# Weaving two batches of a Fourier-layer kernel: chains of one batch between bulk units of the other

## The chip, the cores and the metric

The kernel runs on one core of a Trainium2 chip. The metric is the device time of one execution in microseconds (us); lower is better. The median of three runs before the change is 803.64 us (803.38 to 805.07). All data are 32-bit floats.

Names used below: PE is the matrix engine (TensorE), PEld its weight loads, DVE the vector engine, ACT the scalar (activation) engine, POOL is GpSimd, SP the engine whose queue issues most DMAs. PSUM is the memory that PE writes its products to: 8 banks of 512 floats on each of 128 partitions. SBUF is the main on-chip memory.

## The reference

The input `x` has 2 batches of 56 channels, each a plane of 128 x 128. Two layers of the same form follow one another, with weights of their own:

```
x = x + layer(group_norm(x))

layer(x):                                   # 56 planes of a batch are "tokens"
    xn = instance_norm(x)
    k, q, v = fno(xn, K), fno(xn, Q), fno(xn, V)        # 1 plane -> 8 heads
    attn = softmax(q . k / 128)                          # 56 x 56, each head
    out = fno(attn @ v, P)                               # 8 heads -> 1 plane
    att = instance_norm(out + x);  an = instance_norm(att)
    h = gelu(instance_norm(spectral(an, M0)) + skip)     # exact Gelu
    h = instance_norm(spectral(h, M1)) + skip
    return instance_norm(h) + att

spectral(x, w): rfft2, keep 32 x 16 low modes, multiply by complex w, irfft2
fno(x) = spectral(x) + 1x1 skip
```

Only 32 x 16 complex modes of a plane are kept, so the Fourier transforms are products with small cosine and sine matrices. Attention needs no full planes: the scores come from the modes and from the 56 x 56 Gram matrix of the planes. Full planes are touched where a nonlinearity or a new input needs them: at the load, at the Gelu, and at the end of a layer.

## The kernel before

All work is written out in Python, with no loop left at run time. A compiler pass then orders the instructions of each engine's queue by program order and by its own estimate of when inputs are ready, places tiles, and adds the waits. Each queue runs in order. So the order of the program is a strong hint of the order on an engine, not the order itself.

A batch's `x` stays in SBUF as `X2`: 56 channels on partitions 0 to 55 and, for the other half of the rows, on 64 to 119. `P[b]` holds a batch's working planes. Each stage below runs for one layer `L` and one batch `b`:

- `turned` (line 323): 4 transposes on PE, an ACT copy to `P`, and `bn_stats` on DVE for group statistics; 16 calls turn a batch.
- `modes_stage` (413): group norm from the statistics, the scaling of the plane in four parts (L431 on ACT, L433 on DVE), the transform along the width (L436), a 32 x 32 transpose on DVE (L441), the transform along the height (`to_modes`, L342), the Gram matrix in 128 small products (L460), and square roots for the scores.
- `scale_x` (489): scales `X2` in place for the skip paths (L492 on DVE).
- `heads_stage` (498): scores (L526, L515), softmax, values (L551), attention applied (L596).
- `norms_stage` (607): means and variances of the two instance norms, as sums of squared modes by one-column products (`sums`, L398); then factors, spread over partitions by a product (`rows_of`, L391), the new spectrum (`spectrum`) and the transform back along the height (`inverse`, L358 and L363).
- `gelu_stage` (676): in four blocks, `mixed` rebuilds four tiles of a plane (synthesis along the width L659, 32 products with 64 columns of weights; skip product L669), then Gelu on ACT (L685), the sum of squares on DVE (L686), transposes back (L689), a copy on ACT (L691) and the forward transform (L695).
- `h_stage` (702): modes of the Gelu's output, the second spectral product (`multiply`, L376), its statistics, factors and spectrum, and `inverse`.
- `end_stage` (753): `mixed` again, then for each of 16 tiles a read-back of the layer's input by SP into one of three tiles `xr` (L763), two DVE passes (L765 adds the mixed part, L767 scales by 1/std and adds the read-back), and a store by SP (L769). In layer 0 the result also goes to `X2`, and `turned` starts the next layer.

`prepare` (206) forms the products of the weights on POOL, `relay` (283) turns them, `build` (307, L310) expands them into block matrices on POOL. PSUM has 6 single banks (`bank()`) and one pair, used by `inverse`. `evict` (198) alternates PSUM copies between ACT and DVE. The last lines call the stages: heads and norms of batch 0, then of batch 1; Gelu and `h_stage` of batch 0, then of batch 1; in layer 0 `end_stage` and the next `modes_stage` for each batch in turn, in layer 1 both `end_stage`s. A PE product of 32-bit floats is two instructions in the profile.

Of the kernel before, what the change touches and what calls it, by code (L numbers as in the profile page):

```python
# [26 lines left out]

# [7 lines left out]
F32 = mybir.dt.float32  # L36
# [6 lines left out]
EPS = 1e-5  # L43
# [4 lines left out]
for _name, _n in (  # L48
    ("ident", N), ("fw", 32), ("fh", N), ("gh", 2 * N), ("gw", N), ("group", N), ("dup", N), ("ext", N),
    ("fold", 64), ("raw", 56), ("count", 8), ("syn", 1), ("same", 32), ("m8", 8), ("m16", 16), ("first", 1),  # L50
    ("n2", 1),
):
    _PARTS[_name] = (sum(n for _, n in _PARTS.values()), _n)
# [3 lines left out]
def _constants():  # L57
    pos = np.arange(N)
    rows = 4 * (pos % 32) + pos // 32
    th = 2 * np.pi * np.outer(pos, np.arange(16)) / N  # L60
    ph = 2 * np.pi * np.outer(rows, _KY) / N
    pg = 2 * np.pi * np.outer(pos, _KY) / N
    fw = np.concatenate([np.cos(th), -np.sin(th)], 1) / N
    cy, sy = np.cos(ph), np.sin(ph)
    fh = np.concatenate([cy, -sy, sy, cy], 1) / N
    ghs = []
    for h in (pos.reshape(4, 4, 8), pos.reshape(8, 4, 4)):
        turn = h.transpose(1, 0, 2).reshape(-1)
        cz, sz = np.cos(pg[turn]), np.sin(pg[turn])
        g = np.stack([np.concatenate([cz, -sz], 1).T, np.concatenate([sz, cz], 1).T], 1)  # L70
        ghs.append(np.concatenate([g, g], 0).reshape(N, 2 * N))
# [7 lines left out]
    for r in range(2):  # L79
# [20 lines left out]
        "ident": np.eye(N), "fw": fw, "fh": fh, "gh": ghs[0], "gw": gw, "group": group, "dup": dup, "ext": ext,  # L100
# [6 lines left out]
        "first": (p == 0)[:, None] * 1.0, "n2": np.full((N, 1), 1.0 / N**2),  # L107
    }
    whole = np.concatenate([parts[n] for n in _PARTS] + ghs[1:], 1)
# [23 lines left out]

@with_exitstack
def fno_layers(ctx: ExitStack, tc: tile.TileContext, x, out, weights, small, const):
# [7 lines left out]
    mp = pool("mid", 2)  # L143
# [3 lines left out]
    ps = pool("psum", 6, space=bass.MemoryType.PSUM)  # L147
    pq = pool("pair", 1, space=bass.MemoryType.PSUM)
# [3 lines left out]

    def little(name, shape):
        return sm.tile(shape, F32, name=name)

# [4 lines left out]
    nc.scalar.dma_start(out=ident, in_=const["all"][:, :N])  # L160
    X2 = xp.tile([N, B, 64, N], F32, name="X2")
    xin = x.rearrange("b k (g c r) w -> c b k g (r w)", c=2, r=8)
    for b in range(B):
        for g in range(0, 8, 2):
            V.memset(X2[32:64, b, 8 * g : 8 * g + 16, :], 0.0)
            G.memset(X2[96:128, b, 8 * g : 8 * g + 16, :], 0.0)
# [5 lines left out]
            if (b, g) == (0, 2):  # L172
                nc.scalar.dma_start(out=Ct[:, N:], in_=const["all"][:, N:N_CONST])
# [19 lines left out]
    def grid(flat, n=8):  # L193
        return flat.rearrange("p (t k) -> p t k", t=n)
# [684 lines left out]
```

## Time and profile before

| what | value |
|---|---|
| median of three runs | 803.64 us |
| profiled execution, its own time | 804.52 us |
| its span, first to last instruction | 802.7 us |
| busy: PE, PEld, DVE, ACT, POOL | 563.5, 373.6, 395.9, 189.7, 98.6 us |
| mean granted PE clock | 0.753 |
| moved by DMA | 40.18 MB |

An engine is busy while an instruction of its own runs; the busy times overlap, and their shares of the span are means over stages that are limited by different things. The granted clock is the share of the full PE clock that the chip allowed. A chain line names a step of the chain of work that ended last; "idle before <-" in a group names what ended the wait of the group's engine.

### The profile page before, as it was taken

What the parts mean: (1) busy time and instruction counts of PE and PEld (TensorE: products, weight loads), DVE (VectorE), ACT (ScalarE), POOL (GpSimd) and SP (SyncE); (2) the same over time, 40 slices, a digit from 0 to 9 for tenths busy, and PEclk for the clock granted to TensorE, in tenths of its full rate; (3) what the DMA queues carried; (4) which work ended last, traced back from release to release, by engine and by line L of the source; (5) the groups of instructions that cost most, each with busy time, mean ns of one, the idle gap of its engine ahead of it and who ended that gap; (6) DMA issues with size and microseconds to landing.
All of it is one profiled execution on the core that took longest, in us unless ns stands there. A gap on an engine that the chain in (4) does not pass through costs nothing.

```text
span 802.7 us, 18778 instructions
## 1 busy us (share of the span) xinstructions
PE 563.5 (70%) x8334; PEld 373.6 (47%) x8334; DVE 395.9 (49%) x781; ACT 189.7 (24%) x364; POOL 98.6 (12%) x151
## 2 busy tenths in 40 slices
PE   1576689898797796674476646888979679677810
PEld 1455576867553543432243223767664354353300
DVE  8577813142525344456575556434234434447752
ACT  1405003215044244111111111142324425310000
POOL 9900088000000001400000000000000000000000
PEclk9886859598579589557686667997968959858855
DMA  7920110000000000034403341000000000004565
GB/s 190 209 39 1 30 39 2 2 3 2 0 2 2 2 1 2 1 99 141 136 3 95 107 145 27 4 2 2 2 2 2 2 1 2 2 1 148 181 203 168
DMA packets 21664, 40.18 MB, mean 50 GB/s; under 512 B 4304, under 2 KB 5072, under 8 KB 21584
## 3 DMA queue, kind: packets, MB, share of 16 engines
q1 hardware_dynamic: 20576, 36.98, 16.4%
q10 hardware_dynamic: 1008, 2.01, 0.9%
q8 instruction: 65, 1.06, 0.6%
q14 instruction: 15, 0.12, 0.1%
HBM read 24.03 MB, written 14.68 MB: 48 GB/s over the span
## 4 chain that ended last, share of the span: by engine, by line
PE 47%; DVE 24%; ACT 10%; DMA 9%; issue 5%; SPq 4%; POOL 0%; DVEq 0%; ACTq 0%; POOLq 0%
PE bank L669 7%; PE bank L659 5%; PE bank L526 4%; DVE X L492 4%; PE bank L398 4%; DMA xr<-store 4%; PE pair L358 3%; DMA X<-x 3%; PE bank L596 3%; PE bank L695 3%; PE bank L300 3%; PE bank L342 3%; DVE X L767 2%; DMA xr<-x 2%; DVE P L765 2%
## 5 line engine op out<-in xcount | busy, mean ns | idle before, releaser
L326 PE MATMUL bank<-C,X 120*128 120x120 f32 x256 | 46.6, 341 | 67.2 <-DVE X L767 41.1
L669 PE MATMUL bank<-X,Bs 57*64 57x512 f32 x512 | 91.8, 771 | 0.0
L326 PEld LDWEIGHTS bank<-C,X 120*128 120x128 f32 x256 | 36.7, 182 | 82.8 <-issue 58.0
L686 DVE SCALAR_TENSOR_TENSOR bank<-P 128x512 f32<-128x512 f32 x64 | 42.8, 719 | 50.8 <-ACT P L685 50.6
L329 ACT COPY P<-bank 128x448 f32<-128x448 f32 x64 | 32.9, 541 | 126.3 <-PE bank L326 125.4
L765 DVE SCALAR_TENSOR_TENSOR P<-P,der,bank 128x512 f32<-128x512 f32 x64 | 44.6, 742 | 17.1 <-PE bank L669 17.0
L685 ACT ACTIVATE P<-bank 128x512 f32<-128x512 f32 x64 | 35.4, 601 | 63.8 <-PE bank L669 63.8
L334 DVE BATCH_NORM_STATS2 stats<-P 128x6 f32<-128x448 f32 x64 | 37.7, 620 | 23.0 <-ACT P L329 23.0
L526 PE MATMUL bank<-xf,WU 64*64 64x56 f32 x1024 | 42.2, 247 | 0.0
L526 PEld LDWEIGHTS bank<-xf,WU 64*64 64x64 f32 x1024 | 39.4, 160 | 6.0 <-issue 5.3
L659 PE MATMUL bank<-C,mid 32*64 32x128 f32 x1024 | 35.1, 371 | 8.4 <-DVE P L765 8.4
L203 DVE COPY P<-bank 128x448 f32<-128x448 f32 (+1 forms) x32 | 20.3, 653 | 40.8 <-PE bank L526 40.8
L767 DVE SCALAR_TENSOR_TENSOR P<-P,r,xr 128x512 f32<-128x512 f32 x32 | 23.8, 750 | 31.1 <-DMA xr<-store 31.0
L669 PEld LDWEIGHTS bank<-X,Bs 57*64 57x64 f32 x512 | 21.6, 166 | 37.2 <-issue 37.2
L689 PE MATMUL bank<-C,P 120*128 120x120 f32 x256 | 37.0, 278 | 0.0
L492 DVE TENSOR_TENSOR X<-X,gvr 120x1024 f32<-120x1024 f32 x32 | 36.8, 1213 | 0.3
L691 ACT COPY WT<-bank 128x448 f32<-128x448 f32 x64 | 32.6, 535 | 17.2 <-PE bank L689 17.0
L689 PEld LDWEIGHTS bank<-C,P 120*128 120x128 f32 x256 | 26.3, 142 | 21.1 <-ACT P L685 15.6
L659 PEld LDWEIGHTS bank<-C,mid 32*64 32x64 f32 x1024 | 25.0, 180 | 21.8 <-DVE P L765 14.1
L436 PE MATMUL bank<-P,C 128*32 128x448 f32 x128 | 22.3, 808 | 18.0 <-DVE P L433 17.9
L695 PE MATMUL bank<-WT,C 128*32 128x112 f32 x512 | 25.5, 271 | 13.2 <-ACT WT L691 12.4
L201 ACT COPY P<-bank 128x448 f32<-128x448 f32 (+1 forms) x32 | 17.0, 558 | 68.9 <-PE bank L526 58.6
(229 smaller groups left out, 908.3 us busy)
## 6 DMA issues: line engine op xcount, KB each, us to landing
X<-x SPq DMA_DIRECT2D x16, 448.0 KB
xr<-x SPq DMA_DIRECT2D x64, 112.0 KB
store<-X SPq DMA_DIRECT2D x64, 112.0 KB
xr<-store SPq DMA_DIRECT2D x64, 112.0 KB
out<-P SPq DMA_DIRECT2D x64, 112.0 KB
mid<-weights ACTq DMA_DIRECT2D x2, 544.0 KB
C<-const_all ACTq DMA_DIRECT2D x1, 557.5 KB
X<-gvr SPq DMA_DIRECT2D x8, 32.0 KB
```

The source lines that it names most:

```text
L326: T.transpose(p[:, N * e : N * e + 120], X2[:120, b, 8 * g + 4 * s + e, :], ident[:120, :120])
L334: V.bn_stats(stats[:, 2 * g + s, :], v)
L492: V.tensor_tensor(v, v, _bc(st["gvr"][:120], 1, 8), ALU.mult)
L526: T.matmul(two[k][64 * e : 64 * e + 64, K * a : K * a + K], lhsT=WUv[64 * e : 64 * e + 64, t + k, a, :], rhs=xv[64 * e : 64 * e + 64, t + ...
L659: T.matmul(four[j][64 * c : 64 * c + 64, N * e : N * e + N], lhsT=Z[32 * j : 32 * j + 32, o : o + 64], rhs=C["gw"][32 * j : 32 * j + 32, : ...
L669: T.matmul(four[2 * v + r][64 * c : 64 * c + 64, :], lhsT=Bs[q, :], rhs=X2[q, b, s : s + 4, :].rearrange("p e w -> p (e w)"), start=False, ...
L685: S.activation(h3, four[j], AF.Gelu)
L686: V.scalar_tensor_tensor(four[j], h3, 1.0, h3, ALU.mult, ALU.mult, accum_out=ec[:, n : n + 1])
L689: T.transpose(p[:, N * e : N * e + 120], h3[:120, N * e : N * e + N], ident[:120, :120])
L695: T.matmul(dst, lhsT=C["fw"], rhs=t[:, q], start=(j == 0), stop=True, tile_position=(0, 32 * q), skip_group_check=True,)
L765: V.scalar_tensor_tensor(h3, h3, d["gm1"], four[j], ALU.mult, ALU.add)
L767: V.scalar_tensor_tensor(dst, h3, st["r3"], back, ALU.mult, ALU.add)
```

## The change

The stages become Python generators which yield the estimated PE cost of what they have just issued. `_woven(lead, bulk)` runs a chain of short dependent steps (the lead) and, after each step, issues units of bulk work until their costs add up to what the step yielded. The leads and bulks are, in order: the modes of batch 0 with the turn of batch 1; the modes of batch 1 with the Gram product of batch 0; the rest of Gram and norms of one batch with the Gram product or the scores of the other; the softmax with the values; the mixing with the heads; the norms of batch 0 with all attention of batch 1; the norms of batch 1 with the Gelu of batch 0; `h_chain` of batch 0 with the Gelu of batch 1; `h_chain` of batch 1 with the `end` of batch 0; in layer 0 the modes of layer 1 with the `end` of batch 1.

Besides: PSUM becomes 2 single banks and 3 pairs of banks, and tiles double to 1024 columns (2 x 448 or 2 x 512); all PSUM copies of the bulk go to ACT, two of the four plane scalings too. Synthesis uses 128 columns of weights (`Z` padded to 64 columns a row), 16 products instead of 32 in each block. In layer 0 the turn transposes each half of the channels by itself, so the empty partitions of `X2` need no zeros; they are filled from `x` at the end of the load. Weights and constants are loaded first, on ACT's queue. In `norms_chain` one of three sums of squares goes away. The Gelu's statistics come from `bn_stats`. The layer's last 1/std goes into the factors that precede it (`dcq`, `Be`, `D`, `hs`), so that DVE makes one pass in `end` and POOL adds the read-back. Read-backs are issued two tiles ahead; in the last `end` all eight go ahead, into `X2` of batch 0.

```diff
+def _woven(lead, *bulks):
+    rest = chain(*bulks)
+    for want in lead:
+        while want > 0:
+            cost = next(rest, None)
+            if cost is None:
+                break
+            yield cost
+            want -= cost
+    yield from rest
...
-    ps = pool("psum", 6, space=bass.MemoryType.PSUM)
-    pq = pool("pair", 1, space=bass.MemoryType.PSUM)
+    ps = pool("psum", 2, space=bass.MemoryType.PSUM)
+    pq = pool("pair", 3, space=bass.MemoryType.PSUM)
...
-            V.memset(X2[32:64, b, 8 * g : 8 * g + 16, :], 0.0)
-            G.memset(X2[96:128, b, 8 * g : 8 * g + 16, :], 0.0)
...
+    for b in range(B):
+        nc.sync.dma_start(out=X2[K:64, b], in_=x[b, :8, :64, :])
...
-            if j == 1:
+            if j % 2:
                 S.activation(v, v, AF.Identity, bias=sh, scale=gv)
...
+    def synthesis(A, both, Z):
+        for e in range(4):
+            for j in range(4):
+                o = 64 * (8 * A + 2 * e)
+                T.matmul(
+                    both[j // 2][:, j % 2, N * e : N * e + N], lhsT=Z[32 * j : 32 * j + 32, o : o + N],
+                    rhs=C["gw"][32 * j : 32 * j + 32, :], start=(e == 0), stop=False, tile_position=(32 * j, 0),
+                    skip_group_check=True,
+                )
...
+    def gelu(L, b, st):
...
+        for A in range(6):
+            if A < 4:
+                both = [pair(), pair()]
+                synthesis(A, both, st["Z"])
+                yield 1.0
+            if A > 1:
+                forward(A - 2, 1)
+                yield 0.4
+            for v in range(2):
+                if A < 4:
+                    mixed(L, b, A, v, both[v], st["Bs"])
+                    h3 = at(A, v)
+                    S.activation(h3, both[v].rearrange("p r m -> p (r m)"), AF.Gelu)
+                    for r in range(2):
+                        V.bn_stats(stats[:, 4 * A + 2 * v + r, :], h3[:, 512 * r : 512 * r + 512])
+                    yield 0.9
+                if 0 < A < 5:
+                    turn_back(A - 1, v)
+                    yield 0.8
+            if 0 < A < 5:
+                forward(A - 1, 0)
+                yield 0.4
...
+    def end(L, b, st, stats):
...
+        for n in range(8 if ahead else 2):
+            load(n)
+        late = []
         for A in range(4):
+            both = [pair(), pair()]
+            synthesis(A, both, st["Z"])
+            yield 1.0
+            for v in range(2):
+                n = 2 * A + v
+                mixed(L, b, A, v, both[v], st["Be"])
+                h3 = P[b][:, 1024 * n : 1024 * n + 1024]
+                V.scalar_tensor_tensor(h3, h3, st["hs"], both[v].rearrange("p r m -> p (r m)"), ALU.mult, ALU.add)
+                dst = X2[:, b, 8 * n : 8 * n + 8, :].rearrange("p e w -> p (e w)") if L == 0 else h3
+                G.tensor_tensor(dst, h3, back(n), ALU.add)
+                moved(dst, to, A, v, True, nc.sync)
+                if not ahead:
+                    load(n + 2)
+                yield 0.9
+                late.append(n)
+                if L == 0 and len(late) > 2:
+                    turned(b, late.pop(0), 1, stats)
+                    yield 0.8
...
+        _run(_woven(modes_chain(L, 1, ...), gram(0, s0)))
+        _run(_woven(gram_chain(L, 0, s0), _with(gram(1, s1), scale_x(0, s0))))
+        _run(_woven(gram_chain(L, 1, s1), scores(L, 0, s0)))
+        _run(_woven(softmax_chain(L, 0, s0), values(L, 0, s0)))
+        _run(_woven(mix_chain(L, 0, s0), heads(L, 0, s0)))
+        _run(_woven(
+            norms_chain(L, 0, s0), _with(scores(L, 1, s1), scale_x(1, s1)),
+            _woven(softmax_chain(L, 1, s1), values(L, 1, s1)), _woven(mix_chain(L, 1, s1), heads(L, 1, s1)),
+        ))
+        _run(_woven(norms_chain(L, 1, s1), gelu(L, 0, s0)))
+        _run(_woven(h_chain(L, 0, s0), gelu(L, 1, s1)))
+        _run(_woven(chain(h_chain(L, 1, s1), more), end(L, 0, s0, stats[0])))
+        if L == 0:
+            _run(_woven(modes_chain(1, 0, stats[0], st[1][0]), end(0, 1, s1, stats[1])))
+        else:
+            _run(end(1, 1, s1, None))
```

746 lines of the change are left out of this document (395 added, 351 removed).

## The prediction

> **What bounds the kernel now.** I read the page's engine rows and clock row first, then the shares of the chain, the groups by line, the chain in order of time, and last the busy time by stretch. In the engine rows and the chain's shares no engine is full:
>
> ```profile
> PE 563.5 (70%) x8334; PEld 373.6 (47%) x8334; DVE 395.9 (49%) x781; ACT 189.7 (24%) x364; POOL 98.6 (12%) x151
> PE 47%; DVE 24%; ACT 10%; DMA 9%; issue 5%; SPq 4%; POOL 0%; DVEq 0%; ACTq 0%; POOLq 0%
> ```
>
> PE is busy for 70% of the span and carries under half of the chain; DVE carries 24%, ACT 10% and DMA 9%. So time is lost where one batch's short steps run alone. The next view is stretches (span, then busy PE, PEld, DVE, ACT, POOL, granted clock, DMA share, GB/s): the bulk of the Gelu stage, its follow-up (`h_stage`), one block of four tiles of `end_stage`, the last 81 us, and layer 1's heads with norms.
>
> ```profile
> 223.60:257.60 34.00, 30.06 (x513) 16.35 (x512) 12.53 (x37) 18.75 (x36) 1.07 (x1) 0.92 0.01 1
> 257.60:287.80 30.20, 21.44 (x177) 12.60 (x178) 13.66 (x35) 5.86 (x11) 1.94 (x1) 0.55 0.01 1
> 356.70:370.30 13.60, 6.80 (x102) 4.07 (x102) 7.78 (x12) 2.13 (x4) 0.00 (x0) 0.75 0.44 136
> 722.00:803.00 81.00, 35.16 (x576) 14.83 (x574) 46.30 (x65) 0.00 (x0) 0.00 (x0) 0.69 0.55 174
> 509.30:600.60 91.30, 79.85 (x1570) 63.69 (x1570) 28.98 (x70) 27.88 (x54) 0.00 (x0) 0.82 0.01 2
> 20.00:40.00 20.00, 11.14 (x66) 8.39 (x64) 11.66 (x36) 9.66 (x15) 18.86 (x63) 0.87 0.90 209
> ```
>
> The Gelu bulk keeps PE busy 30.06 of 34.0 us, at clock 0.92. Its follow-up needs 30.2 us at clock 0.55. A block of `end_stage` takes 13.6 us with PE half idle. The last 81 us run at 174 GB/s; the first load reached 209. The chain shows why (start, us, what):
>
> ```profile
> 13.08 15.24 DMA X<-x
> 31.89 0.60 DVE mv L415
> 47.96 0.53 ACT xf L201
> ...
> 257.60 3.67 DVE WU L706 x4
> 261.32 3.31 PE bank L342 x8
> 268.48 3.16 PE bank L398 x32
> 287.81 0.58 ACT P L685
> ...
> 356.70 1.94 PE bank L659 x64
> 365.86 2.47 DMA xr<-x
> ```
>
> The first modes stage stands behind X's load and ends at 48.5. `h_stage` is a string of single steps, and the next Gelu starts at 287.81, after it. In `end_stage` every block waits for a read-back issued only after the block's own stores.
>
> **The change part by part.** *Weaving* moves nearly everything, so I cost sections: each is as long as the largest of its PE work at full clock, its chain, and its DMA. PE rates come from stretches that ran near full clock:
>
> ```profile
> 233.85 1.09 PE bank L659 x57
> 234.94 1.09 PE bank L669 x8
> 242.61 1.09 PE bank L669 x8
> 517.87 2.12 PE L526 MATMUL bank<-xf,WU 64*64 64x56 f32 x64
> 520.09 0.98 PE L515 MATMUL bank<-P,xf 128*64 128x224 f32 x8
> 524.66 3.60 PE L551 MATMUL bank<-WT,xf 64*64 64x512 f32 x28
> 533.31 5.51 PE L596 MATMUL bank<-P 56*64 56x56 f32 x256
> 544.82 3.12 PE L398 MATMUL bank<-C,P 128*56 128x1 f32 x32
> 168.61 1.05 PE pair L358 x8
> 48.26 7.67 PE L460 MATMUL bank<-P 128*64 128x56 f32 x256
> 48.74 9.17 DVE L492 TENSOR_TENSOR X<-X,gvr 120x1024 f32<-120x1024 f32 x8
> 214.84 3.52 PE bank L300 x16
> L659 PE MATMUL bank<-C,mid 32*64 32x128 f32 x1024 | 35.1, 371 | 8.4 <-DVE P L765 8.4
> L695 PE MATMUL bank<-WT,C 128*32 128x112 f32 x512 | 25.5, 271 | 13.2 <-ACT WT L691 12.4
> L326 PE MATMUL bank<-C,X 120*128 120x120 f32 x256 | 46.6, 341 | 67.2 <-DVE X L767 41.1 <-POOL eps L175 14.9 <-DVE P L351 7.6
> L310 POOL TENSOR_TENSOR WU<-tc,C 128x1024 f32<-128x1024 f32 x8 | 15.3, 1943 | 50.3 <-PE bank L342 42.6 <-ACT tc L304 7.6
> L685 ACT ACTIVATE P<-bank 128x512 f32<-128x512 f32 x64 | 35.4, 601 | 63.8 <-PE bank L669 63.8
> L765 DVE SCALAR_TENSOR_TENSOR P<-P,der,bank 128x512 f32<-128x512 f32 x64 | 44.6, 742 | 17.1 <-PE bank L669 17.0
> L767 DVE SCALAR_TENSOR_TENSOR P<-P,r,xr 128x512 f32<-128x512 f32 x32 | 23.8, 750 | 31.1 <-DMA xr<-store 31.0
> L334 DVE BATCH_NORM_STATS2 stats<-P 128x6 f32<-128x448 f32 x64 | 37.7, 620 | 23.0 <-ACT P L329 23.0
> L492 DVE TENSOR_TENSOR X<-X,gvr 120x1024 f32<-120x1024 f32 x32 | 36.8, 1213 | 0.3
> L685 ACT ACT_TABLE_LOAD x4 | 5.1, 1283 | 0.1
> ```
>
> Gelu: one of four blocks repeats every 7.67 us (234.94 to 242.61). In it 57 of the synthesis' 64 instructions (L659) take 1.09, so all take 1.25. It becomes 32 instructions with 128 columns of weights instead of 64, which no row shows on 32 rows: from 0.6 (time goes with the instruction count) to 1.25 (with the columns loaded). I take 1.0, nearer the columns, since 19 ns for each instruction is already a small part of the 0.3 us that one lasts. The forward transform (L695) goes from 32 short instructions, 25.5 us over 16 blocks, to 16 of twice the width: 0.8 to 1.6, taken as 1.15. A block is then 7.67 - 0.25 - 0.45 = 7.0 and a Gelu bulk 28. Norms lose 16 of 48 one-column products (32 take 3.12, so 1.5 each time, and the zero-mean count goes). All told PE loses about 0.25 x 32 + 0.45 x 16 + 1.5 x 4 = 21 us.
>
> The sections, in the new order. (1) Start: 48, as now. The memsets that held the first loads back go, but 3.7 MB of X and about 1.3 of weights and constants must land before batch 0 is whole, 24 us at 209 GB/s, and 3.7 more for batch 1; batch 1's turn hides inside. Layer 0's turn doubles its transposes, halved in rows and run side by side: from equal to 8.9 us more for each batch, hidden by the load. (2) Modes of batch 1, 16.6 (31.89 to 48.5), then two relays, about 5 each (3.52 of products, then small copies), over the Gram product (7.67): 27. (3) Gram of batch 1 over the other's chain, with the scaling (L492, 8 x 1.21) on DVE: 10. (4) Scores: 4 x 2.12 + 4 x 0.98 plus the chain's products: 14. (5) Values 32/28 x 3.60 plus transposes: 7. (6) Heads 5.51 plus mixing: 9. (7) Norms of batch 0, PE 7 (3.12, two times 1.05, and small products), over 4 to 6 of batch 1: 35. (8) Norms over Gelu: 28 + 7 = 35. (9) h over Gelu: 28 + 8.5 = 36.5; at full clock h's own products are 1.75, 1.2, 3.1 and two times 1.05. (10) h and three relays over `end` of batch 0: `end` has 4 x (1.0 + 1.95) + 8.9 (62 of 64 turns at 0.14), h 8.5, relays 6, together 35 on PE; DVE about 38 (8 x 1.5, 16 x 0.62, h about 11 and relays 5); 7.3 MB, at 205 GB/s, just under the load's 209, 36 (42 at 174). I take 40. (11) Modes over `end` of batch 1: DMA 36, so 38. (12) Layer 1's modes over Gram: 17. (13) Items 3 to 9 again: 146.5. (14) h over `end`, then `end`: 14.7 MB at 205 GB/s, 72, which also hides h.
> Sum: 48 + 27 + 146.5 + 40 + 38 + 17 + 146.5 + 72 = 535.
>
> No section reaches its bound. Today's two densest stretches take 34.0 for 30.06 of PE and 91.3 for 79.85: 13 and 14% more. I charge 14% on the 487 after the start: 68, so 603.
>
> *Moved among engines.* DVE loses the second pass of `end` (L767, 64 at 0.75, 48 us), half the evictions, one of two plane scalings and the two-operand Gelu sum, replaced by `bn_stats` at about 0.7. POOL gains 32 adds; the row for 1024 columns says 1.94 each, 15.5 for each `end` beside 36 of DMA. Zero if covered; if the add of the last tile shows, 1.2 more at the tail. ACT takes the evictions: from 0.6 for 512 columns (L685), 1.2 for 1024 and 1.0 for 896, so 17.6 in a Gelu section of 35. Gelu now alternates with square roots, and each switch loads a table (1.28): up to 6 in each of four sections, 31 us on ACT, hidden by ACT's idle half, all exposed without it. The adds add a wait: an add queues on POOL behind the weight builds (4 x 1.94 for WU), its store on SP behind the add, and the read-backs behind that store; those are issued two tiles ahead, so up to two tiles' time is covered. Transfers twice as large halve SP's issues. *Folding 1/std* takes a reciprocal, a product and a `[1,56]` step out of h: under 1 us, inside (9).
>
> Here the Trainium skill speaks against the change: "GPSIMD Engine Reference", Performance versus the Vector engine, has elementwise adds about twice as slow on GpSimd, with 2293 against 4497 ns at 2048 columns. The trace agrees in kind: 1.21 us on DVE against 1.94 on POOL for 1024. By the rows POOL has 15.5 us for each `end`, by the page an estimated 18; both lie under its DMA, and the sum stays.
>
> **The rivals.**
> *Leads stand in line.* Each chain step now queues behind a bulk unit of 0.7 to 1.4 us on DVE or ACT, and bulk waits in PE's queue behind a step whose input is late; the compiler orders queues by its own estimate. It already moves code: the scaling, written after the norms, ran at 48.74. Without PE's share, h is 30.2 - 8.5, norms about 19 - 7 and modes 16.6 - 6.7, four of each: 175 us. Half of it exposed again adds 87: 692. For: in the woven Gelu DVE has about 26 of 35 us of work (16 sums at 0.7, 4 copies, and the chain's 12). Against: each lead is spaced by units of about its own latency.
> *The clock stays at its present mean.*
>
> ```profile
> core 0: 802.7 us, clock 0.753
> ```
>
> The stretches above show 0.55 where PE has gaps and 0.92 where it is dense. If weaving leaves gaps, PE's work stays 563 - 21 = 542 busy; with 14% that is 618, plus PE's idle 35 at the start and 48 in the tail: 701. Against: in the woven order PE has other work in every section. The page "TensorE: Matmul & The Clock Gate" of the Trainium skill, section "A second HAM failure mode: psum-queue depth-cycling", says that a PE which cycles through PSUM with small gaps falls back to half rate again and again; three slots of two banks are such a cycle. The Gelu bulk, which cycles six banks, shows 0.92, so the trace does not bear it out so far.
> *The ends keep their period.* If add and store still hold the read-back, layer 0's ends stay at 4 x 13.6 = 54 each and the last stage at 81: 38 more, 643.
> *PSUM in pairs serializes, slower than before.* 49 pairs are taken for each batch and layer, 196 in all, in three slots; Gelu and `end` hold two of them while the third turns. If PE waits out each eviction (1.2, from ACT's and DVE's rows), 196 x 1.2 = 235: 840. It decides from (804 - 605)/196 = 1.02 us for each pair. Against: a slot comes round two units later, and units of 0.8 to 2 us of PE work lie between.
>
> **How the numbers follow.** The sum is made against the profiled execution (span 802.7, its own time 804.5, so 1.8 outside; the median is 803.6): 603 + 2 = 605. Chances: forecast, 560 to 645, 0.48; the ends' rival 0.07; better, 530 to 560, if the 14% is too much, 0.07; leads in line 0.20; clock 0.11; pairs 0.06; 0.01 for no change. Low end 548: synthesis at 0.6 and forward at 0.8 take another 18 over 32 and 16 blocks, and over half of the 14% (39) goes. High end 715: the leads' rival with most of the table loads exposed (692 + 23). Faster by over 0.2% (about what this measurement can tell from no change) 0.93, within it 0.01, slower 0.06.
>
> **What would show it.** Right: a Gelu block every 6 to 7.5 us with the other batch's steps inside; clock over 0.85; the stretch after layer 1's second Gelu under 80 us; POOL near 160 us busy; synthesis at 32 instructions in about 1.0. Wrong: PE idle before synthesis on ACT's Gelu (pairs); PE idle on DVE's small steps of another batch (leads); clock near 0.75; PE idle on POOL or DMA in the ends.

## The result and the profile after

The changed kernel takes 573.83 us (median of four runs, 573.12 to 574.03); the kernel before took 804.36 in the same comparison. The ratio is 0.712, 95% interval 0.709 to 0.716: 231 us, or 29%, are gone. The forecast was 605, range 548 to 715.

The page of the kernel after: busy time of the engines, granted clock by slice, and shares of the chain that ended last.

```profile
PE 468.0 (82%) x7110; PEld 323.5 (57%) x7110; DVE 334.5 (59%) x577; ACT 191.1 (33%) x238; POOL 181.9 (32%) x190
PEclk9999699887999998977577959987799999899587
...
PE 48%; DVE 25%; DMA 8%; ACT 7%; issue 5%; POOL 4%; SPq 1%; POOLq 1%; ACTq 0%; DVEq 0%
```

PE is busy 82% of the span where it was 70%. It also does its work in less time: 468.0 us instead of 563.5, for 7110 instructions instead of 8334. Part of that is the clock, 0.882 on average in the profiled execution against 0.753. PE still carries only 48% of the chain, DVE a quarter: chains and bulk now alternate on the path instead of chains standing alone.

The next view is busy time by stretch of the kernel after (stretch, span, busy PE, PEld, DVE, ACT, POOL with instruction counts, granted clock, DMA share, GB/s). The borders are: batch 1's turn nearly done; first Gelu; layer 0's ends; layer 1's scores; layer 1's Gelu; last h chain and ends.

```profile
0.00:61.00 61.00, 30.09 (x310) 19.79 (x311) 29.74 (x73) 19.86 (x22) 17.61 (x63) 0.98 0.72 153
61.00:169.00 108.00, 97.86 (x2019) 79.02 (x2016) 57.56 (x92) 32.91 (x45) 46.89 (x52) 0.89 0.09 21
169.00:241.00 72.00, 69.40 (x875) 41.62 (x870) 50.09 (x101) 40.26 (x47) 3.70 (x15) 0.98 0.01 2
241.00:349.00 108.00, 84.85 (x911) 57.48 (x913) 78.57 (x110) 23.42 (x31) 58.68 (x31) 0.75 0.45 127
349.00:437.00 88.00, 79.83 (x1696) 62.38 (x1700) 36.34 (x67) 30.79 (x40) 16.76 (x12) 0.90 0.07 19
437.00:511.00 74.00, 70.24 (x902) 42.22 (x893) 50.55 (x100) 40.25 (x47) 0.99 (x2) 0.98 0.01 3
511.00:571.60 60.60, 35.67 (x426) 20.94 (x426) 31.69 (x38) 3.58 (x7) 37.29 (x16) 0.76 0.69 220
```

The two Gelu stretches (169 to 241, 437 to 511) have PE busy for 96 and 95% at clock 0.98. The stretches with attention (61 to 169, 349 to 437) come to 91% at about 0.9. Loose are the start, layer 0's ends (79%, clock 0.75) and the tail (59%), which are also the three that move data. The chain of the kernel after in order of time (start, us, what) names what stands in those three:

```profile
1.64 11.70 DMA sm<-small
26.53 7.91 DVE stats L373 x15
...
270.68 9.08 issue
279.80 3.84 POOL WU L341 x2
...
527.03 4.48 DMA xr<-store
535.54 4.08 DMA xr<-store
```

At the start it is the loads and fifteen statistics in a row on DVE; in the first end 9.08 us with nothing but issue, in which POOL stands in front of two expansions of weight matrices (PE itself is without work for 4.0 us of it), then these expansions; in the tail the read-backs.

Kernels are compared below by their ratios, and a difference of two ratios, times 804, is given in us. Three executions were disturbed, one of the kernel without weave (712.9 us) and two of the one with moved relays (582.7 and 582.4), and the figures below leave them out, but the profiles of these two kernels come from such executions, so their stretches, which two expectations use, are good for sizes only.

### The profile page after: what moved, and what is told of

It reads as the page before. It is cut to its first block, busy times and chain, and to the rows that moved or that the text cites. A ratio compares the mean times of both kernels' runs of the same rounds, so it can differ in the third digit from the quotient of the medians.

```text
span 571.6 us, 15727 instructions
## 1 busy us (share of the span) xinstructions
PE 468.0 (82%) x7110; PEld 323.5 (57%) x7110; DVE 334.5 (59%) x577; ACT 191.1 (33%) x238; POOL 181.9 (32%) x190
## 4 chain that ended last, share of the span: by engine, by line
PE 48%; DVE 25%; DMA 8%; ACT 7%; issue 5%; POOL 4%; SPq 1%; POOLq 1%; ACTq 0%; DVEq 0%
PE pair L766 6%; PE pair L751 5%; PE pair L595 4%; PE pair L801 4%; PE pair L689 4%; DVE X L550 4%; DVE stats L373 4%; PE bank L576 3%; PE bank L511 3%; PE bank L789 2%; DVE P L916 2%; DMA X<-store 2%; PE bank L483 2%; PE bank L386 2%; DMA sm<-small 2%
## 5 line engine op out<-in xcount | busy, mean ns | idle before, releaser
L821 DVE BATCH_NORM_STATS2 stats<-P 128x6 f32<-128x512 f32 x64 | 40.4, 677 | 20.2 <-ACT P L819 20.1
L916 DVE SCALAR_TENSOR_TENSOR P<-P,hs,pair 128x1024 f32<-128x1024 f32 x32 | 40.0, 1271 | 19.9 <-PE pair L766 19.8
L918 POOL TENSOR_TENSOR X<-P,xr 128x1024 f32<-128x1024 f32 x16 | 39.4, 2466 | 31.1 <-DVE P L916 20.0
L550 DVE TENSOR_TENSOR X<-X,gvr 120x1024 f32<-120x1024 f32 x32 | 48.9, 1558 | 0.0
L511 PE MATMUL bank<-P 128*64 128x56 f32 (+1 forms) x1024 | 38.7, 243 | 0.0
L511 PEld LDWEIGHTS bank<-P 128*64 128x64 f32 (+1 forms) x1024 | 37.1, 158 | 2.2 <-issue 1.9
L766 PE MATMUL pair<-X,Be 57*64 57x512 f32 x256 | 38.2, 692 | 0.0
L766 PE MATMUL pair<-X,Bs 57*64 57x512 f32 x256 | 37.6, 628 | 0.0
L595 PEld LDWEIGHTS pair<-xf,WU 64*64 64x64 f32 x1024 | 33.3, 138 | 5.0 <-issue 4.1
L595 PE MATMUL pair<-xf,WU 64*64 64x56 f32 x1024 | 36.1, 223 | 0.0
L801 PE MATMUL pair<-C,P 120*128 120x120 f32 x256 | 35.4, 282 | 0.7 <-ACT P L819 0.5
L341 POOL TENSOR_TENSOR WT<-tc,C 128x1024 f32<-128x1024 f32 x8 | 26.5, 3344 | 20.0 <-ACT tc L335 11.9
```

Source lines behind the costliest of these rows:

```text
L511: T.matmul(p[u : u + m, :K], lhsT=P[b][:, K * i : K * i + m], rhs=plane[b][:, i, :], start=(i < 2), stop=(i == N - 1), tile_position=(0, u ...
L550: V.tensor_tensor(v, v, _bc(st["gvr"][:120], 1, 8), ALU.mult)
L595: T.matmul(p[64 * e : 64 * e + 64, k, K * a : K * a + K], lhsT=WUv[64 * e : 64 * e + 64, t + k, a, :], rhs=xv[64 * e : 64 * e + 64, t + k, ...
L766: T.matmul(p[64 * c : 64 * c + 64, r, :], lhsT=Bs[q, :], rhs=X2[q, b, s : s + 4, :].rearrange("p e w -> p (e w)"), start=False, stop=True, ...
L801: T.transpose(p[:, r, N * e : N * e + 120], h3[:120, o : o + N], ident[:120, :120])
L821: V.bn_stats(stats[:, 4 * A + 2 * v + r, :], h3[:, 512 * r : 512 * r + 512])
```

## The experiments

All edits are to the kernel after, and all compute the whole result.

**No weave.** `_woven` runs the lead to its end and then the bulk; every other edit stays.

```diff
 def _woven(lead, *bulks):
-    rest = chain(*bulks)
-    ...
-    yield from rest
+    yield from chain(lead, *bulks)
```

> The changed kernel with one edit: each lead is issued whole, then its bulks, so the program order is again one stage after the other; engines, PSUM pairs, folding and read-backs stay. Theory A (the order written into the program is what overlaps the chains): the 175 us of chain latency that the prediction counted come back at least in the places where nothing else is in flight, 660 to 740 us, granted clock back under 0.82, PE busy about as in the changed kernel plus slow clock (480 to 530 us). Theory B (the compiler orders by readiness anyway, and the gain comes from the moves among engines, the pairs and the read-backs): 574 to 610 us, clock 0.86 or more.

Measured: 702.68 us, ratio 0.869 (0.866 to 0.872). So the order of the program does make the overlap; the compiler's pass doesn't find it by itself. The weave is worth 0.157, 126 us, of the 231, and the rest of the change 105.

**Two PSUM pairs instead of three.** The banks are split as four single ones and two pairs.

```diff
-    ps = pool("psum", 2, ...)
-    pq = pool("pair", 3, ...)
+    ps = pool("psum", 4, ...)
+    pq = pool("pair", 2, ...)
```

> The changed kernel with 4 single banks and 2 pairs in place of 2 and 3. Theory A (three slots are enough because a unit of PE work covers an eviction of 1.0 us): the third slot is what hides it, so with two the synthesis of each of the 32 blocks waits for the last eviction of the block before, about 2 us each, and each of the other 68 pairs loses up to 1 us: 64 + 30 or so, 640 to 680 us, with PE waiting in L751 and L801 for ACT. Theory B (PE is held by other things, eviction is never late): 574 to 585 us.

Measured: 610.69 us, ratio 0.756 (0.753 to 0.757), 35 us slower: between the two. The row of the synthesis' weight loads on PE in `end` for the kernel with two pairs, and then the same row of the kernel after (busy, mean ns, idle before and its releasers):

```profile
L751 PEld LDWEIGHTS pair<-C,WT 32*128 32x128 f32 x512 | 33.4, 228 | 27.4 <-DVE P L916 16.1 <-DVE WT L406 4.8 <-issue 3.6
```

```profile
L751 PEld LDWEIGHTS pair<-C,WT 32*128 32x128 f32 x512 | 23.6, 225 | 21.6 <-DVE P L916 7.2 <-issue 5.3 <-DVE WT L406 3.1
```

The loads wait 16.1 us for DVE's pass instead of 7.2: with two slots PE can't begin the next pair while the last one is read. The third pair of banks matters, and 196 pairs make it 0.18 us each. But waiting is the smaller part: PE's idle time grows by only 7 us, while PE is busy 498.4 us instead of 468.0 for the same 7110 instructions. The two woven Gelu sections of the kernel with two pairs, by stretch (columns as above; in the kernel after they are the rows 169 to 241 and 437 to 511):

```profile
170.20:255.20 85.00, 79.09 (x861) 45.84 (x860) 50.42 (x101) 40.20 (x46) 1.10 (x3) 0.94 0.01 1
452.50:541.40 88.90, 82.44 (x926) 48.90 (x918) 50.84 (x99) 40.91 (x47) 0.99 (x2) 0.92 0.01 2
```

They take 85.0 and 88.9 us instead of 72.0 and 74.0, which is most of the loss, and the granted clock in them is 0.94 and 0.92 instead of 0.98. The mean over the whole kernel, 0.889 against 0.882, doesn't show this. By an estimate from these rows (69.4 x 0.98 / 0.94 = 72.4, and the same for the second) the clock makes 3 to 5 of the 10 to 12 us that PE is busy longer in each; the rest stays open.

**The read-back added on DVE.**

```diff
-                G.tensor_tensor(dst, h3, back(n), ALU.add)
+                V.tensor_tensor(dst, h3, back(n), ALU.add)
```

> The changed kernel with the read-back added on DVE instead of POOL. Theory A (POOL's add shuts out DVE instructions with two SBUF inputs: a [128,1] product that takes 0.16 us took 2.33 at 298.95, scale_x has a mean of 1.56 against a median of 1.21; and the last end is 8 adds of 2.35 in a row): DVE takes 32 x 1.2 = 39 us more, but the stalls (11 us in scale_x, about 10 in small steps) and 8 us of POOL after the last DVE pass go: 560 to 574 us. Theory B (DVE is the fuller engine in the ends and the add was rightly moved): 580 to 600 us.

Measured: 577.64 us (573.78 to 581.79), ratio 0.716 (0.711 to 0.721): no difference that can be told. An add takes 1.31 us on DVE in layer 0 and 1.22 in layer 1, on POOL 2.47 and 2.35. So the move of the adds to GpSimd, by itself, buys nothing here, nor does it cost.

**Synthesis in 64-column products again**, twice as many of half the width.

```diff
-                o = 64 * (8 * A + 2 * e)
-                T.matmul(both[j // 2][:, ...], lhsT=Z[..., o : o + N], ...)
+                for c in range(2):
+                    o = 64 * (8 * A + 2 * e + c)
+                    T.matmul(both[j // 2][64 * c : 64 * c + 64, ...], lhsT=Z[..., o : o + 64], ...)
```

> The changed kernel with the synthesis in 32 products with 64 columns of weights again, 64 instructions in place of 32 for each block. Theory A (the columns loaded set its time: 32 instructions took 1.12 in the changed kernel where 1.0 was forecast, 64 took 1.25 before): 0.1 to 0.15 us for each of 32 blocks, 575 to 580 us. Theory B (the instruction count sets it, at 19 ns each, and the wide form is hidden by something else): 64 instructions take 0.6 us more, 590 to 595 us.

Measured: 573.68 us, ratio 0.711 (0.708 to 0.713): no difference. One block of synthesis in the timeline of the kernel with 64 columns (start, us), and one in that of the kernel after:

```profile
193.59 1.21 PE L752 MATMUL pair<-C,P 32*64 32x128 f32 x64
```

```profile
181.68 1.17 PE L751 MATMUL pair<-C,P 32*128 32x128 f32 x32
```

64 instructions take 1.21 us, 32 take 1.17. So the time doesn't go with the count; what the two forms share is the columns of weights that they load, 64 x 64 and 32 x 128. The Trainium skill says this of the weights ("TensorE: Matmul & The Clock Gate", LDWEIGHTS (loading the stationary operand)): the load goes with the columns, whatever the rows. This pair of rows agrees as to the columns; the rows are 32 in both.

**The start: weights formed on GpSimd alone.**

```diff
-    par, d, cpt, tcs = prepare(0, V, G)
+    par, d, cpt, tcs = prepare(0, G, G)
```

> Edit: the products of the weights for layer 0 are formed on GpSimd alone, not half of them on DVE. Theory A (the start is late because DVE's queue holds these products, which wait 19.1 us for the constants' load, ahead of the first statistics): the first group norm comes 3 to 6 us earlier and the kernel takes 568 to 571 us. Theory B (the start waits for the planes of batch 0 to arrive, whatever DVE does; the products then only take longer on GpSimd and delay the first relays): 574 to 580 us.

Measured: 570.89 us (568.08 to 571.93), ratio 0.707 (0.705 to 0.710), 4 us faster than the kernel after, as theory A has it. DVE's timeline of the kernel after shows what the first statistics stood behind (start, us, operation, idle before and its releaser):

```profile
20.24 0.73 DVE L270 TENSOR_TENSOR stage<-stage,C 128x544 f32<-128x544 f32 x1 [19.09 <-DMA C<-const_all]
...
26.45 7.99 DVE L373 BATCH_NORM_STATS2 stats<-P 128x6 f32<-128x448 f32 x15
34.47 0.59 DVE L458 BATCH_NORM_AGGREGATE mv<-stats 128x2 f32<-128x96 f32 x1
```

and in the kernel with this edit:

```profile
18.18 2.20 DVE L373 BATCH_NORM_STATS2 stats<-P 128x6 f32<-128x448 f32 x4 [5.15 <-ACT P L368]
...
29.96 0.59 DVE L458 BATCH_NORM_AGGREGATE mv<-stats 128x2 f32<-128x96 f32 x1
```

With DVE's queue blocked by L270, which waits 19.09 us for the constants, the statistics pile up; without it they follow the planes as these arrive, and the group norm starts at 29.96 instead of 34.47. This version beats both kernels, if by little.

**The last adds shared by DVE and GpSimd.**

```diff
-                G.tensor_tensor(dst, h3, back(n), ALU.add)
+                (V if ahead and n % 2 else G).tensor_tensor(dst, h3, back(n), ALU.add)
```

> Edit: in the last end every second add of the read-back runs on DVE, the others on GpSimd. Theory A (GpSimd's eight adds of 2.35 us are what ends last: DVE is done with its passes at 560, GpSimd at 566.9): the tail shortens by 4 to 6 us, 568 to 570 us. Theory B (the end is set by the eight 448 KB stores on the way out, and they would only queue): 573 to 575 us.

Measured: 573.66 us, ratio 0.711 (0.709 to 0.714): no difference, theory B. The trace of the kernel after had pointed to GpSimd, which adds without a pause until 566.9; its timeline:

```profile
548.34 18.52 POOL L918 TENSOR_TENSOR P<-P,X 128x1024 f32<-128x1024 f32 x8 [6.21 <-DVE P L916]
```

With the adds shared, the last of them don't end earlier. The last add of each engine in that kernel's timeline:

```profile
562.66 3.26 POOL L918 TENSOR_TENSOR P<-P,X 128x1024 f32<-128x1024 f32 x1 [0.30 <-DVE P L916]
564.95 2.06 DVE L918 TENSOR_TENSOR P<-P,X 128x1024 f32<-128x1024 f32 x1
```

GpSimd ends at 565.9, DVE at 567.0. In this execution the last end begins 2.5 us later (DVE's first pass at 549.43 instead of 546.92), the adds on DVE put off its own passes (the last ends at 564.9 instead of 560.1), and side by side the adds run longer, 2.81 us on average on GpSimd and 1.73 on DVE, where they take 2.35 and 1.22 with one engine adding alone. So sharing gains nothing; whether the kernel would be shorter if the adds did end earlier, this run can't say.

**Read-backs of the last end from ACT's queue.**

```diff
-                moved(back(n), raw, n // 2, n % 2, False, nc.sync)
+                moved(back(n), raw, n // 2, n % 2, False, nc.scalar if ahead else nc.sync)
```

> Edit: the read-backs of the last end are issued from ACT's queue, not from SP's, where 16 of them take 11.6 us to issue (543.0 to 554.7) ahead of the first of the last stores. Theory A (the last stores wait for SP's queue: first issued at 555.3, though the first add ends at 550.7): stores start 4 us earlier and the kernel takes 568 to 571 us. Theory B (GpSimd's adds, back to back from 548.3 to 566.9, or the DMA engines at 250 to 350 GB/s set the end, whoever issues): 573 to 575 us.

Measured: 575.76 us (572.81 to 577.43), ratio 0.713 (0.710 to 0.716): no difference. SP, free of the read-backs, now waits 19.2 us for adds, in ten waits, while GpSimd adds without a pause from 551.0 to 569.5. So moving the adds to DVE, sharing them and moving the read-backs each gain nothing. But the last add ends at 567.4, 567.0 and 569.5 in these three kernels against 566.9 in the kernel after, and the execution 4 to 6 us behind it in all four: none of the trials ended the adds earlier. Whether the adds, the transfers or the h chain ahead of them set the tail stays open. The stretches of the kernel after in the tail (columns as above):

```profile
511.00:543.00 32.00, 20.70 (x234) 13.07 (x234) 21.80 (x30) 3.58 (x7) 18.78 (x8) 0.73 0.57 179
543.00:555.00 12.00, 11.64 (x146) 6.28 (x148) 5.85 (x5) 0.00 (x0) 6.66 (x3) 0.86 0.88 250
555.00:571.60 16.60, 3.34 (x48) 1.59 (x46) 4.04 (x4) 0.00 (x0) 11.85 (x6) 0.75 0.78 276
```

From 543 on, 250 to 276 GB/s pass with DMA engines busy for 78 to 88%. Before that it is 179 GB/s: the h chain is at work there, and read-backs into three tiles `xr` wait for a tile to come free. Whether more tiles would help wasn't tried.

**Gelu sections unwoven.** Norms of batch 1, Gelu 0, h of batch 0, Gelu 1, one after the other, in both layers.

```diff
-        _run(_woven(norms_chain(L, 1, s1), gelu(L, 0, s0)))
-        _run(_woven(h_chain(L, 0, s0), gelu(L, 1, s1)))
+        _run(chain(norms_chain(L, 1, s1), gelu(L, 0, s0)))
+        _run(chain(h_chain(L, 0, s0), gelu(L, 1, s1)))
```

> Edit: the four sections that pair a norms or h chain with a Gelu of the other batch run one after the other, all other sections stay woven. Theory A (what the weave saves is the sum of what it covers in each section): in the kernel without any weave the norms chain of batch 1, Gelu 0, the h chain and Gelu 1 of layer 0 stand between 191 and 287 us, 96 us, where the woven ones take 72 (169 to 241): 24 us a layer, 48 in all, so 615 to 628 us. Theory B (an unwoven section gets its time back through a higher granted clock, or moves its wait elsewhere, so that sections don't add up): under 600 us.

Measured: 622.37 us, ratio 0.771 (0.769 to 0.774), 47 us slower, theory A. The clock doesn't make it up: it falls to 0.844.

**Ends unwoven.**

```diff
-        _run(_woven(chain(h_chain(L, 1, s1), more), end(L, 0, s0, stats[0])))
+        _run(chain(h_chain(L, 1, s1), more, end(L, 0, s0, stats[0])))
...
-            _run(_woven(modes_chain(1, 0, ...), end(0, 1, s1, stats[1])))
+            _run(chain(modes_chain(1, 0, ...), end(0, 1, s1, stats[1])))
```

> Edit: in layer 0 the h chain with the relays and end 0, and the modes of layer 1 and end 1, run one after the other; all other sections stay woven. Theory A (sections add up): without any weave this stretch takes 133 us (287 to 420), woven 108 (241 to 349): 25 us more, 593 to 605 us. Together with the Gelu sections that would leave about 55 of the 126 us to the attention of both layers. Theory B (not additive: DVE, GpSimd and the read-backs set the ends, woven or not): under 585 us.

Measured: 617.15 us, ratio 0.765 (0.762 to 0.767), 42 us slower, more than either theory said. The expectation overlooked that the first of these lines runs in both layers: layer 1's h chain and end 0 are unwoven too. ACT's first Gelu of layer 1 begins with this row in the timeline of the kernel after, and then of this one:

```profile
440.78 1.28 ACT L819 ACT_TABLE_LOAD   x1 [2.74 <-PE pair L766]
```

```profile
465.47 1.28 ACT L819 ACT_TABLE_LOAD   x1 [2.56 <-PE pair L766]
```

Up to there 24.7 us are lost, which is layer 0's part, as expected (25); the other 21 of the span's 46 (617.7 against 571.6) come after it, in layer 1. Gelu sections and ends account for 89 of the weave's 126 us; that the other 37 lie in attention and the modes is only the difference.

**The relays moved** from end 0 to the Gelu of batch 1.

```diff
-        _run(_woven(h_chain(L, 0, s0), gelu(L, 1, s1)))
+        _run(_woven(chain(h_chain(L, 0, s0), more), gelu(L, 1, s1)))
...
-        _run(_woven(chain(h_chain(L, 1, s1), more), end(L, 0, s0, stats[0])))
+        _run(_woven(h_chain(L, 1, s1), end(L, 0, s0, stats[0])))
```

> Edit: the three relays of layer 1's weights follow the h chain of batch 0, woven into the Gelu of batch 1, instead of the h chain of batch 1, woven into end 0. Theory A (in end 0 the relays' own chain PE, DVE, PE, ACT stops TensorE's queue, 9.08 us of issue at 270, and holds GpSimd's expansion of the matrices, which waits 9.12 us for ACT ahead of a read-back add, up to 286; in the Gelu section they cost only their 9 us of TensorE): 5 to 10 us faster, 564 to 569 us. Theory B (the Gelu section, with TensorE busy for 96%, pays what the end gains, or end 0 is bound by its transfers and DVE): 572 to 578 us.

Measured: 575.97 us (573.77 to 578.21), ratio 0.713 (0.710 to 0.717): no difference, theory B. Three rows of ACT's timeline mark the first Gelu, the first copy of end 0's turn and the square root at the start of batch 1's modes in layer 1, in the kernel after and then in this one:

```profile
171.29 1.28 ACT L819 ACT_TABLE_LOAD   x1 [1.63 <-PE pair L766]
248.68 0.91 ACT L371 COPY P<-pair 128x896 f32<-128x896 f32 x1 [13.14 <-PE pair L365]
349.37 0.29 ACT L466 ACTIVATE gv<-gv,eps 128x1 f32<-128x1 f32 x1
```

```profile
180.11 1.28 ACT L819 ACT_TABLE_LOAD   x1 [1.63 <-PE pair L766]
269.92 0.91 ACT L371 COPY P<-pair 128x896 f32<-128x896 f32 x1 [6.73 <-PE pair L365]
359.95 0.29 ACT L466 ACTIVATE gv<-gv,eps 128x1 f32<-128x1 f32 x1
```

The ends shrink from 100.7 to 90.0 us, and the stretch with the Gelu grows from 77.4 to 89.8: what was waited out in one place is paid in the other, where PE has no room.

**No read-ahead**: a tile's read-back is issued with the tile, behind the store before it.

```diff
-        for n in range(8 if ahead else 2):
+        for n in range(8 if ahead else 0):
...
+                if not ahead:
+                    load(n)
                 G.tensor_tensor(dst, h3, back(n), ALU.add)
                 moved(dst, to, A, v, True, nc.sync)
-                if not ahead:
-                    load(n + 2)
```

> Edit: in three of the four ends the read-back of a tile is issued with the tile itself, behind the store of the tile before, instead of two tiles ahead; the last end is as it was. Theory A (a read-back of 448 KB takes 3 to 5 us from its issue and GpSimd then waits for each one, 8 tiles in 3 ends): 20 to 50 us slower, 594 to 624 us. Theory B (the weave gives each tile a period of about 5 us, in which the read-back is hidden anyway): 574 to 580 us.

Measured: 584.85 us, ratio 0.724 (0.721 to 0.728), 9.5 us slower: between the theories. A tile's period in a woven end hides most of a read-back.

**Neither weave nor read-ahead.**

> Edit: no weave anywhere, and no read-back ahead in three of the four ends, both edits of the runs before together. With the weave the lost read-ahead cost 11 us (585 against 574); without the weave the kernel took 703 us, and its two layer 0 ends about 39 us each, against 55 and 58 in the kernel before. Theory A (in an unwoven end nothing else covers a read-back, so that the same edit is worth more there: the ends go back towards the old block of 13.6 us, 10 to 17 us more in each of three): 730 to 755 us, and read-ahead explains a third to a half of the 101 us that are not the weave's. Theory B (the parts add up: the ends got shorter by fewer DVE passes and larger tiles, and read-ahead is worth the same 11 us): 709 to 720 us.

Measured: 719.29 us, ratio 0.889 (0.884 to 0.895), 16 us over the kernel without weave: within theory B's bounds, though somewhat more than with the weave. So 89 us of the 231 (1 less 0.889) come neither from the weave nor from reading ahead. This kernel also shows one Gelu bulk and the h chain behind it, unwoven, by stretch (columns as above), and below them the two woven Gelu sections of the kernel after:

```profile
204.20:232.00 27.80, 26.35 (x322) 15.12 (x320) 14.68 (x25) 16.25 (x17) 0.00 (x0) 0.96 0.01 1
232.00:253.00 21.00, 10.14 (x90) 7.68 (x92) 9.02 (x25) 3.58 (x7) 0.11 (x1) 0.62 0.00 1
```

```profile
169.00:205.00 36.00, 35.43 (x476) 21.43 (x475) 25.78 (x52) 21.87 (x25) 3.28 (x13) 1.00 0.01 2
205.00:241.00 36.00, 33.97 (x410) 20.20 (x402) 24.32 (x50) 18.39 (x23) 0.42 (x2) 0.95 0.01 1
```

The parts take 27.8 and 21.0 us, 48.8 together, with PE busy for 36.5. Woven they take 36.0, with PE busy for 34 to 35.4. A woven section is as long as the PE work of its two parts, and the chain is free apart from its own products.

## Why the prediction was right, and where its terms were not

The forecast's cause held: chains stood alone, and weaving hides them behind bulk. The weave alone is over half of the gain. The sum came out 31 us too high, and its terms missed by more than that in both directions; that they cancel so far is luck. The border at 349 in the view above lies in the middle of section 12, so layer 0's ends are parted from it here, at the first row below (the Gram product of batch 0 in layer 1), and section 12 from section 13 at the second (the last copy of batch 1's modes). Some first scores of section 13, from 348.9 on, run within section 12.

```profile
337.08 7.25 PE L511 MATMUL bank<-P 128*64 128x56 f32 x170
359.73 0.53 ACT L498 COPY xf<-bank 128x448 f32<-128x448 f32 x1 [1.51 <-PE bank L386]
```

The stretches against the numbered sections of the forecast:

| stretch | forecast's sections | forecast, before the 14% | measured |
|---|---|---|---|
| 0 to 61 | 1 | 48 | 61.0 |
| 61 to 169 | 2 to 7 | 102 | 108.0 |
| 169 to 241 | 8, 9 | 71.5 | 72.0 |
| 241 to 337 | 10, 11 | 78 | 96.0 |
| 337 to 360 | 12 | 17 | 23.0 |
| 360 to 511 | 13 | 146.5 | 151.0 |
| 511 to 571.6 | 14 | 72 | 60.6 |
| sum | | 535 | 571.6 |

- **The 14% for friction (68 us) was the step that failed most.** Over the bare sum the kernel lost 48 us in six stretches and won 11 in the tail, 37 in all. The charge was read from stretches of the kernel before that were 13 and 14% over their PE work; woven Gelu sections are 4% over theirs (72.0 against 69.4), since one batch's gap is the other's turn. Nor was friction even: next to nothing in sections 8 and 9, 13 us at the start and 18 in the ends. The flat charge covered two losses that the forecast hadn't seen.
- **Start: 48, measured 61.** The forecast left the start as it was. But constants loaded first leave DVE's queue standing on them; 4 us of the 13 are shown to be that. And three relays of layer 0's weights run, of which section 2 counts two: the first follows batch 0's modes, which end at 55.4 instead of 48.5, and in PE's order batch 1's last transposes (59.36) stand behind its products (57.65). That this, and the sharing of PE, ACT and DVE between batch 1's turn, which the forecast hid, and batch 0's modes, make the rest is argued, not shown.
- **Gelu: block 7.0, bulk 28; measured 27.8** unwoven. It was right as a sum, less so in its parts: synthesis 1.17 instead of 1.0, near the upper of the forecast's two cases (time goes with the columns), so that its new form buys next to nothing. The forward transform, forecast at 1.15, is two runs of 0.58 or 0.59.
- **Ends: 40 and 38; measured 96 for the two.** Bytes weren't the limit there (134 GB/s on average, DMA share 0.46). The term that failed is the relays, put at 6 us of PE. Rows of the kernel after (start, us): the last small step of batch 1's h chain, a turn that waits for end 0's last add, and the inverse transform, whose input the first row completes.

```profile
273.84 0.19 DVE L876 TENSOR_TENSOR WU<-dcq,bank 1x56 f32<-1x56 f32 x1
286.00 1.86 PE L365 MATMUL pair<-C,X 120*128 120x120 f32 x8 [0.91 <-POOL X L918]
287.79 3.04 PE L401 MATMUL pair<-WU,C 64*128 64x224 f32 x16
```

The inverse has its input at 274.0 and runs at 287.8. In PE's order the relays' products (275.85 to 285.1) and this turn stand in front of it, and the turn waits for an add (283.60) that POOL makes only after two expansions, which themselves wait for the relays. End 1, which needs the inverse, begins its synthesis at 293.7. So what the relays cost is their place in the queues and not their 6 us of PE; by the rough sizes of the kernel with moved relays, the ends are some 11 us shorter without them. In end 1 an expansion of `WT` (6.08 us from 320.05) holds an add whose input is ready at 320.65 until 326.09; the forecast set only the expansions of `WU` ahead of an add. What else is in the 18 us stays open.

- **Tail: 72, measured 60.6.** Of the 14.7 MB 13.3 passed in this stretch, at 220 GB/s, not 205; the first three tiles had been read back at 371 to 387 already. That the transfers set the tail and cover the h chain, as the forecast had it, isn't shown: from 522 to 543 the chain goes from an add to a read-back (4.48 and 4.08 us) and on to the next add, and after that no trial ended the adds earlier.
- **POOL: about 160 us busy forecast, measured 181.9.** An add takes 2.35 to 2.47 us, not the 1.94 of the expansion; the last end's eight adds are 18.5 together. The estimate by the Trainium skill's page "GPSIMD Engine Reference", Performance versus the Vector engine, 18, was the better one. It cost nothing, as the forecast said of either.

```profile
L918 POOL TENSOR_TENSOR X<-P,xr 128x1024 f32<-128x1024 f32 x16 | 39.4, 2466 | 31.1 <-DVE P L916 20.0 <-DVE gs L463 3.8 <-DMA xr<-x 3.1
```

- **Table loads hidden:** right. In the kernel after six loads of 1.28 us stand ahead of the Gelu's calls, and ACT is busy for 40 of the 72 us of layer 0's two sections.

The rivals. *Leads in line* (692): fell; the Gelu sections run at their PE work. In one place it is what happened: the inverse behind the relays, above. *The clock stays* (701): fell, but its premise held. Over these kernels the clock goes with how dense PE is: 0.79 with neither weave nor read-ahead (PE busy 70% of the span), 0.844 and 0.846 with a part unwoven (78%), 0.882 woven (82%), and in stretches 0.96 for an unwoven Gelu, 0.62 for the h chain behind it. It is no full rule: in the first 61 us PE is busy 49% at 0.98. So the weave pays twice: PE is busy 504.7 us in the kernel with neither and 468.0 in the kernel after, for the same 7110 instructions. *The ends keep their period* (643): fell for the tail, 20 us below its old 81; layer 0's ends, 96 us, are nearer to this rival's 108 than to the forecast's 78, but not by its mechanism: of the idle time before their adds GpSimd waits 3.1 us for read-backs and 20.0 for DVE's passes. Reading ahead is 9.5 us of it all, in three ends. *Pairs serialize* (840): fell. Even with one slot fewer a pair costs 0.18 us more, not the 1.02 from which it would decide. The rule of the Trainium skill in "TensorE: Matmul & The Clock Gate", A second HAM failure mode: psum-queue depth-cycling, which spoke for a lower clock with pairs, is borne out in part: the means of the kernels, 0.882 with three pairs and 0.889 with two, don't show it, but in the woven Gelu sections the clock is 0.98 with three and 0.94 and 0.92 with two. *Better, 530 to 560*: not reached.

Of the 231 us, then, 126 are the weave, about 16 the read-ahead (9.5 once woven), and about 89 everything else together. Shorter Gelu bulks (34.0 to 27.8, four times) make about 25 of these, read from stretches; where the rest lies wasn't tried part by part; tried alone in the woven kernel, wide synthesis and the adds on GpSimd are worth nothing that can be measured, and the third pair of banks 35 us.

## What to carry to other kernels

Cost a woven section as the PE work of both its parts at the clock that a dense PE gets, and look for friction first where data moves or where a queue mixes work that waits with work that doesn't. Where the program's order is what overlaps two chains, write that order out, and give PSUM one slot more than the two parts hold, as far as one trial shows (35 us here). When a trial on what a trace shows to be last changes nothing, look whether it ended that work earlier at all.

## What the hardware did that was not expected

Small steps on DVE can take as long as a whole add on GpSimd. In the timeline of the kernel after (start, us, operation), two steps of 56 and 128 values beside the adds that started just before them:

```profile
262.71 2.34 POOL L918 TENSOR_TENSOR X<-P,xr 128x1024 f32<-128x1024 f32 x1 [2.59 <-DVE f L863]
262.80 2.26 DVE L864 TENSOR_TENSOR f<-c,f 56x1 f32<-56x1 f32 x1
...
298.93 2.35 POOL L918 TENSOR_TENSOR X<-P,xr 128x1024 f32<-128x1024 f32 x1 [3.83 <-DVE gs L463]
298.95 2.33 DVE L464 TENSOR_TENSOR gv<-gs 128x1 f32<-128x1 f32 x1
```

At the start of the kernel, with no such add beside it, L464 takes 0.16 us:

```profile
36.19 0.16 DVE L464 TENSOR_TENSOR gv<-gs 128x1 f32<-128x1 f32 x1
```

Both steps end with the add. The Trainium skill has the rule ("SBUF — State Buffer", SBUF: two separate sides): a DVE operation with two SBUF inputs and a GpSimd operation that reads SBUF exclude each other, and the one that comes second waits for the whole of the other. These rows agree, whatever the size of the waiting one. In the pass of `end`, which reads one of its inputs from PSUM, nothing of the kind shows: 1.271 us on average, beside all these adds.

The scaling on DVE (two SBUF inputs) and GpSimd's expansion of `WT` lengthen each other likewise. Groups of the kernel after:

```profile
L550 DVE TENSOR_TENSOR X<-X,gvr 120x1024 f32<-120x1024 f32 x32 | 48.9, 1558 | 0.0
L341 POOL TENSOR_TENSOR WT<-tc,C 128x1024 f32<-128x1024 f32 x8 | 26.5, 3344 | 20.0 <-ACT tc L335 11.9 <-PE bank L386 8.1
L341 POOL TENSOR_TENSOR WU<-tc,C 128x1024 f32<-128x1024 f32 x8 | 15.4, 1945 | 35.6 <-ACT tc L335 33.4 <-PE pair L401 2.2
```

The scaling took 1213 ns on average in the kernel before and takes 1558 now (its median is still 1210, so it is single ones that wait, up to 3357); the expansion of `WT` takes 3344 where that of `WU`, away from the scaling, takes 1945. With the adds on DVE the scaling still takes 1513, so the adds are little of it. A move to GpSimd of work with SBUF inputs is no free move, then, if DVE has two-input work at the same time.
